# An attention and mixture-of-experts layer on one core: who rounds the posts' weights, the order of the last batch's units, and a written order for the end

## The chip, the cores and the metric

One Trainium2 chip, one of its cores. The metric is the device time of one execution in microseconds. PE is the tensor engine, DVE the vector engine, ACT the scalar engine, POOL (Pool) the GpSimd engine, SP the engine whose queue issues all the DMAs.

## The reference

Four sequences (batches) of 2048 tokens with 256 channels, in float32. Cut to what matters:

```
x = x + attention(layernorm(x))      # 16 heads of 16 channels; scale 1/16; + b_o + layernorm(x)
x = x + ffn(layernorm(x))
ffn(y): scores = softmax(y @ w_gate.T)               # 8 experts in 4 groups of 2
        two groups, then the two best experts inside them, by scores + expert_bias
        routed row r = token of expert index flat_idx[r], scaled by its weight
        h = silu(row @ w1[e]) * (row @ w3[e]); routed_out = h @ w2[e]
        shared = silu(y @ sw1.T) * (y @ sw3.T) @ sw2.T
        out = shared.at[flat_idx].add(routed_out)    # flat_idx are expert numbers, 0 to 7
```

As `flat_idx` holds expert numbers, the routed part reads rows 0 to 7 of the input and adds to rows 0 to 7 of the output alone. So it comes down to sums over all 16384 choices (two for each of 8192 tokens) of a sigmoid of a row's scaled product, weighted, for eight rows and eight experts.

## The kernel before, in words

The tokens are cut into chunks of 512, four to a batch, and the heads into four groups of four. A *unit* is one batch, one group and one chunk of queries against all 2048 keys of its batch; there are 64. A unit needs three streams on PE:

- the *maxima*: 64 products `mx` of 128 queries by 512 keys, each reduced by DVE to a row maximum `ms` (`mx_stream`, `finish_mx`). The negated maxima are transposed and sent by DMA into row 63 of the unit's query tile `qst`, where they act as an offset;
- the *scores*: 64 products `st` of 128 keys by 512 queries, each followed by ACT's exponential into `et` (`do_s`);
- the *values*: 16 steps of four products `av` (`do_a`), whose 17th row a head is the sum of the exponentials.

Maxima run about 1.4 units ahead of the scores; a unit's scores need all of its maxima. Queries and keys are split into a high and a low rounded part, so that a product in the fast format keeps its precision. Keys of one batch and group (2 MB) lie in one of two tiles `kst`, values in `vst`, queries in one of three `qst`; `load_unit` and `load_v` issue the loads. In the first three batches the units go group by group, so that one key load serves four units. In the last batch the first three chunks go group by group, and then the fourth chunk goes through all groups, with a third place for keys made of four other tiles (`spare_k`).

Beside the units runs other work: layer norms and projections of the next batch (`norm`, `qkv`: `pt_x`, `pp`, `pv`), and a *post* for each finished chunk (`post`: `post_first` divides by the sums, `post_a` makes the output product `po`, residual, second layer norm and its transpose `pt_x`; `route` makes gate products `lgT` and the ranking on DVE; `shared` makes `pa`, `pb`, `pd`). Each of these is a generator that yields what it needs. A planner orders PE, DVE, POOL and ACT while the program is built: it keeps an estimated clock for each engine (`plan.clock`), holds a window of the next steps, and improves their order by a seeded random search; `LATE` sets how much a late post costs in that search, for the last so many units of work. SP's queue is ordered by the framework.

`setup` loads the posts' four weights (`wt`, into two buffers) and splits them: ACT rounds the high part, POOL subtracts for the low part.

After the last unit, `last_heads` turns the last four heads, and `finish` alternates two generators, `front` (post_a of the last chunk, `route`, then the experts, `moe`) and `behind` (`post_b`, the shared part of the last chunk). Only their emission is alternated; the framework's scheduler orders the engines. `moe` counts choices (`m_cs`, `m_pc`, `m_tot`, `m_cum`), then goes through 16 groups of choices. For a group: `ob` and `ow` (the choice's one-hot rows, DVE and POOL), `mo` and `oT` (turned by PE, copied by DVE), `mu` (products with the tables), `mth` (their sigmoid: half by four ACT instructions, half by DVE and one ACT instruction), and `pg` (weighted sums in one bank). A step of the loop does ob, ow, mo and oT of group g, mu and mth of g-1, pg of g-2. Then `m_sg`, `m_ph`, `m_gb`, `m_pr`, `m_s`, `m_po`, and the last write.

Nearly every instruction is issued through one helper, line 56, so the profile's groups are told apart by tile names.

Of the kernel before, what the change touches and what calls it, by code (L numbers as in the profile page):

```python
# [33 lines left out]
LEAD = 6  # L34
HORIZON = 46
COMMIT = 10
LATE = 0.01, 0.1, 16
TURNS = 1600
WARM = 1.5
NET = 6  # L40
# [366 lines left out]
def body(tc, B, L, cols, x, wqkv, bqk, wst, bst, bv, wo, bo, wg, w1, w2, w3, sw1, sw2, sw3, ebias, cst, pad, out):  # L407
# [21 lines left out]
    def need(kind, ns=0, *tiles, more=0, act=940):  # L429


        return kind, ns, tiles, more, act

    def gate(open_):

        return "g", open_, (), 0, 0
# [123 lines left out]
    def to_channels(src, name, keep=None, fast=False, out=None):  # L560

        h, l = out or hl(f"t_{name}")
        if not fast:
            for c in range(2):
                f = keep[:, c, :] if keep is not None else sb.tile([P, QC], F32, tag="qkf", name=f"f_{name}{c}", bufs=2)
                pt = stile(f"pt_{name}{c}")
                for i in range(TQ):
                    T.transpose(pt[:, i * P:(i + 1) * P], src[:, i, c * P:(c + 1) * P], ident)
                S.copy(f, pt)
                G.tensor_copy(h[:, c, :], f)  # L570
                G.tensor_tensor(l[:, c, :], f, h[:, c, :].bitcast(F32), ALU.subtract)
                if c == 0:
                    yield need("s1", 436, act=470)
            return h, l
        for c in range(2):
            pt = mtile(f"pt_{name}{c}")
            for i in range(TQ):
                T.transpose(pt[:, i * P:(i + 1) * P], src[:, i, c * P:(c + 1) * P], ident)
            S.copy(keep[:, c, :], pt)
# [250 lines left out]
    def moe():  # L830
# [17 lines left out]
        pg = ps_av.tile([P, QC], F32, tag="av", name="pg")  # L848
        GR = 8
        NG = NR // GR  # L850
        ows, oTs, ths = {}, {}, {}

        def ranges(r0, r1):
            n = r1 - r0
            V.tensor_tensor(ge[:, r0:r1], K["rows"][:, r0:r1].unsqueeze(2).broadcast_to([P, n, E + 1]),
                            cum[:, 0:E + 1].unsqueeze(1).broadcast_to([P, n, E + 1]), ALU.is_ge)
            V.tensor_tensor(oe[:, r0:r1], ge[:, r0:r1, 0:E], ge[:, r0:r1, 1:E + 1], ALU.subtract)

        def pick(g):
            sl = slice(g * GR, (g + 1) * GR)  # L860
            ob = sb.tile([P, GR, E, 8], BF16, tag="x", name=f"ob_{g}", bufs=2)
# [5 lines left out]
            obf = ob.rearrange("p r e j -> p (r e j)")  # L867
            for q in range(GR // 2):
                T.matmul(pt[:, q * P:(q + 1) * P], obf[:, q * P:(q + 1) * P], identb, start=True, stop=True)
            oT = oTs[g] = sb.tile([P, GR // 2, P], F32R, tag="hi", name=f"oT_{g}", bufs=3)  # L870
            V.tensor_copy(r2(oT), pt)
# [56 lines left out]
    def post_first(b, c, nh=H):  # L928
# [63 lines left out]
    last = {}  # L992

    def post_last():

# [67 lines left out]
            V.tensor_tensor(xv, pd, xv, ALU.add)  # L1063
        write(ch, x1)

    def post_b(ch, n, x1, x2T, x2hl, rt, eng=G, hhl=None):

        hT = f4(f"hT_{n}")
        hhl = hhl or hl(f"hT_{n}")
        for m in range(2):  # L1070
            pa = mtile(f"pa_{n}_{m}")
            mm3(pa, W["s_1"], x2hl, slice(m * P, (m + 1) * P), slice(0, QC))
            th = sb.tile([P, QC], F32, tag="sth", name=f"th_{n}_{m}", bufs=2)
            S.activation(th, pa, AF.Tanh, scale=0.5)
            if eng is G:
                yield
            if eng is None:
                S.copy(hT[:, m, :], pa)
                G.tensor_tensor(th, th, K["ones"][:, 0:1].broadcast_to([P, QC]), ALU.add)
                G.tensor_tensor(th, th, hT[:, m, :], ALU.mult)  # L1080
            else:
                V.scalar_tensor_tensor(th, th, 1.0, pa, ALU.add, ALU.mult)
            yield
            next(rt, None)
# [3 lines left out]
            if eng is None:  # L1088
                S.mul(hT[:, m, :], pb, 0.5)
                G.tensor_tensor(hT[:, m, :], hT[:, m, :], th, ALU.mult)  # L1090
            else:
                V.scalar_tensor_tensor(hT[:, m, :], pb, 0.5, th, ALU.mult, ALU.mult)
            S.copy(hhl[0][:, m, :], hT[:, m, :])
            (eng or G).tensor_tensor(hhl[1][:, m, :], hT[:, m, :], hhl[0][:, m, :].bitcast(F32), ALU.subtract)
            yield
            next(rt, None)
# [12 lines left out]
    def spare(i):  # L1109

        t = kst[1 - kslot[kset[-1]]][:, i // 2, (i % 2) * 2 * QC:(i % 2 + 1) * 2 * QC]
        return t.rearrange("p (t n) -> p t n", t=2)

    def post(b, c):
# [9 lines left out]
    def finish():  # L1124
# [6 lines left out]
        def behind():  # L1131
            while "q" not in last:
                yield
            yield from post_b(*last["q"], iter(()), None)

        live = [front(), behind()]
        while live:
            for g in list(live):
                try:
                    next(g)  # L1140
                except StopIteration:
                    live.remove(g)


    queue, posts, side, norms, sums, firsts = (deque() for _ in range(6))
# [23 lines left out]
    def load_unit(u):  # L1169

        b, g, c = units[u]
        if fresh[u] and u != len(units) - 3:
            src = kd[b][4 * g:4 * g + 4].rearrange("(p h) r n -> (h r) p n", p=2)
            if kslot[kset[u]] == 2:
                spare_k.extend(hl("k_hq", "hq"))
                spare_k.extend(sb.tile([P, 2, QC], F32R, tag="x", name=f"k_x{i}", bufs=2) for i in range(2))
# [241 lines left out]
    def setup():  # L1418
# [359 lines left out]
```

## Time and profile before

| | |
|---|---|
| median of 3 runs | 3067.62 us (3067.2 to 3068.33) |
| profiled execution, its own time | 3064.53 us |
| its span, first to last instruction | 3062.7 us |
| mean granted PE clock | 0.986 |
| busy: PE, DVE, ACT, POOL | 2982.9, 2823.3, 2420.8, 649.9 us |
| last maximum reduced / last unit's exponentials begin | about 2931 / 2936.7 us |
| last value product ends / last group's pg ends | 2971.1 / 3056.6 us |

The busy times are unions of the instructions' spans on an engine; a matmul's end is modelled and matmuls overlap, so PE's share is not its share of peak. Stretches in the profile are cut in microseconds from the start of the span. The scores of unit 48 begin at 2251.9, of unit 52 at 2445.3, of unit 58 at 2685.9.

### The profile page before, as it was taken

The page shows a single profiled execution, that of the slowest core. Times are in us where ns is not written, and L with a number is a line of the kernel's source. Part 1 is how long each engine was busy: PE and PEld are TensorE (multiplying, and loading weights), DVE is VectorE, ACT ScalarE, POOL GpSimd, SP SyncE. Part 2 cuts the span into 40 slices and gives each one's busy share as a digit, 9 for nine tenths or more (in the row PEclk, how much of TensorE's full clock was granted, in tenths as well). Part 3 has the DMA queues.
Part 4 walks back from the last instruction along what each step waited for, and adds up shares of the span by engine and source line. Part 5 has one row for each costly group of instructions (what it writes and reads, how often), then busy time and mean ns, then how long its engine had stood idle before and what let it go on. Part 6 is the DMA issues. An engine that isn't in the chain of part 4 may idle for free.

```text
span 3062.7 us, 52745 instructions
## 1 busy us (share of the span) xinstructions
PE 2982.9 (97%) x19427; PEld 1359.8 (44%) x19427; DVE 2823.3 (92%) x5129; ACT 2420.8 (79%) x4745; POOL 649.9 (21%) x662
## 2 busy tenths in 40 slices
PE   7989999999999999999999999999999999999988
PEld 5434444444444444444444444444444444444436
DVE  7879999999999999999999999999999999999926
ACT  5578888888878878788888778888778788887774
POOL 5233223133213112110221220000222200023313
PEclk9899999999999999999999999999999999999998
DMA  5555645343121312221121200201121101011200
GB/s 157 184 156 151 167 114 162 94 140 112 51 94 40 115 32 88 64 79 69 44 86 39 72 25 20 90 22 69 45 75 49 69 25 58 31 54 40 77 26 15
DMA packets 144797, 237.32 MB, mean 77 GB/s; under 512 B 17115, under 2 KB 73563, under 8 KB 140379
## 3 DMA queue, kind: packets, MB, share of 16 engines
q1 hardware_dynamic: 144539, 233.96, 24.3%
q8 instruction: 153, 2.51, 0.3%
q14 instruction: 105, 0.86, 0.1%
HBM read 138.38 MB, written 111.80 MB: 82 GB/s over the span
## 4 chain that ended last, share of the span: by engine, by line
PE 80%; DVE 15%; DMA 1%; issue 1%; ACT 1%; POOL 1%; SPq 0%; POOLq 0%; ACTq 0%; DVEq 0%
PE av L56 29%; PE mx L56 20%; PE st L56 19%; DVE ms L56 11%; PE pp L56 3%; PE pd L56 2%; PE pv L56 1%; PE po L56 1%; PE pt_x L56 1%; PE pa L56 1%; PE pb L56 1%; PE mu L56 1%; ACT et L56 1%; PE pg L56 1%; DVE eq L56 1%
## 5 line engine op out<-in xcount | busy, mean ns | idle before, releaser
L56 DVE TENSOR_REDUCE ms<-mx 128x1 f32<-128x512 f32 x4096 | 2521.6, 682 | 135.0 <-PE mx L56 100.5
L56 ACT ACTIVATE et<-st 128x512 f32<-128x512 f32 x4096 | 2139.9, 611 | 440.4 <-PE st L56 288.2
L56 PE MATMUL mx<-kst,qst 63*128 63x512 f32 x3984 | 1222.7, 442 | 27.9 <-ACT et L56 10.6
L56 PE MATMUL st<-qst,kst 64*128 64x512 f32 x4032 | 1221.9, 440 | 7.3 <-DMA qst<-mt 3.4
L56 PE MATMUL av<-et,vst 128*32 128x512 f32 x8192 | 1098.4, 607 | 0.8 <-ACT ao L56 0.6
L56 PEld LDWEIGHTS mx<-kst,qst 63*128 63x128 f32 x3984 | 577.7, 186 | 605.8 <-DVE ms L56 289.8
L56 PEld LDWEIGHTS st<-qst,kst 64*128 64x128 f32 x4032 | 580.8, 186 | 556.1 <-DVE ms L56 278.9
L56 PEld LDWEIGHTS av<-et,vst 128*32 128x32 f32 x8192 | 164.0, 108 | 328.4 <-issue 307.7
L56 POOL TENSOR_TENSOR aT<-aT,rb 128x512 f32<-128x512 f32 (+1 forms) x32 | 40.9, 1285 | 571.3 <-DMA rb<-rd 570.9
L56 POOL CAST hi<-qkf 128x512 fp32r<-128x512 f32 x56 | 34.2, 610 | 328.3 <-ACT qkf L56 314.3
L56 POOL TENSOR_TENSOR lo<-qkf,hi 128x512 fp32r<-128x512 f32 x64 | 82.1, 1283 | 22.9 <-ACT hi L56 13.2
L56 ACT ACTIVATE qkf<-pp,b_qk 128x512 f32<-128x512 f32 x64 | 44.0, 687 | 53.8 <-PE pp L56 53.6
L56 POOL TENSOR_TENSOR th<-th,cs 128x512 f32<-128x512 f32 x32 | 33.5, 1046 | 222.8 <-ACT th L56 222.8
L56 POOL TENSOR_TENSOR rs_b<-rs_b,nhalf 128x4 f32<-128x4 f32 x16 | 16.3, 1017 | 279.7 <-DVE rs_b L56 279.7
L56 POOL TENSOR_TENSOR hT<-hT,th 128x512 f32<-128x512 f32 x32 | 41.0, 1281 | 123.7 <-ACT hT L56 47.4
L56 POOL TENSOR_TENSOR x<-x,xl 128x256 f32<-128x256 f32 x64 | 46.4, 755 | 16.8 <-ACT xl L56 16.8
L56 POOL TENSOR_TENSOR x<-x,b_o 128x256 f32<-128x256 f32 x64 | 45.5, 740 | 0.0
L56 ACT ACTIVATE xl<-x,rs_a 128x256 f32<-128x256 f32 x64 | 33.4, 594 | 11.1 <-DVE rs_a L56 11.0
L56 ACT COPY ao<-av 128x512 f32<-128x512 f32 x63 | 37.9, 601 | 3.0 <-PE av L56 2.0
L56 POOL TENSOR_TENSOR th<-th,sg 128x512 f32<-128x512 f32 x30 | 38.9, 1296 | 2.4
L56 ACT ACTIVATE th<-pa 128x512 f32<-128x512 f32 x32 | 19.2, 599 | 24.5 <-PE pa L56 24.2
L56 ACT ACTIVATE x<-x,rs_b 128x256 f32<-128x256 f32 x64 | 33.2, 597 | 6.6 <-DVE rs_b L56 6.6
(406 smaller groups left out, 2177.3 us busy)
## 6 DMA issues: line engine op xcount, KB each, us to landing
kst<-kd SPq DMA_DIRECT2D x16, 2048.0 KB
qst<-qd SPq DMA_DIRECT2D x63, 512.0 KB
qd<-hi SPq DMA_DIRECT2D x64, 256.0 KB
kd<-hi SPq DMA_DIRECT2D x64, 256.0 KB
ad<-ao SPq DMA_DIRECT2D x63, 256.0 KB
vst<-vd SPq DMA_DIRECT2D x19, 664.0 KB
vd<-vt SPq DMA_DIRECT2D x32, 332.0 KB
x<-x SPq DMA_DIRECT2D x16, 512.0 KB
```

What stands on the lines that cost most here:

```text
L56: r = f(*a, **k)
```

## The change

Five parts.

1. `split` with an engine given lets that engine (POOL) round the high part too. `setup`, and `post_first` ahead of its reciprocal, first pass a gate `later()`: nothing goes on until the planner's PE clock has moved by 12 us.
2. The last batch's units go chunk by chunk, four groups each. Every unit then needs other keys than the one ahead, and the places for keys go 0, 2, 1, 0, 2, 1 and so on. There are 16 key sets in the last batch.
3. `LATE` counts for the last 3 units of work, not 16.
4. `finish` runs in the written order on POOL, DVE, PE and ACT. `post_b` does its products and ACT's parts first; its ten POOL operations wait until the experts' loop has begun, and go one to a step. The transposes' low parts (`low`) come later, after the gate products. The copy of `m_cum` is taken out of its bank as `m_cm`.
5. The experts' loop has four stages: step g does pg of g-3, ob and ow of g, mu and mth of g-2, mo and oT of g-1. `ow` shares the six buffers of `et`.

```diff
-LATE = 0.01, 0.1, 16
+LATE = 0.01, 0.1, 3
...
+    def later(ns=12000):
+        t = plan.clock["PE"] + ns
+        return gate(lambda: plan.clock["PE"] > t)
...
     def split(name, tmp, out=None, eng=None):
-        S.copy(h, tmp)
+        (S.copy if eng is None else eng.tensor_copy)(h, tmp)
         (eng or V).tensor_tensor(l, tmp, h.bitcast(F32), ALU.subtract)
...
     def to_channels(src, name, keep=None, fast=False, out=None):      # its fast part
+        pts = []
         for c in range(2):
-            pt = mtile(f"pt_{name}{c}")
+            pts.append(mtile(f"pt_{name}{c}"))
...
-            S.copy(h[:, c, :], pt)
-            V.tensor_tensor(l[:, c, :], pt, h[:, c, :].bitcast(F32), ALU.subtract)
-            yield
+            S.copy(keep[:, c, :], pts[c])
+        for c in range(2):
+            S.copy(h[:, c, :], pts[c])
+        def low():
+            for c in range(2):
+                V.tensor_tensor(l[:, c, :], pts[c], h[:, c, :].bitcast(F32), ALU.subtract)
+        last["low"] = low
+        yield
...
+        cm = sb.tile([P, E + 1], F32, tag="m_cm", name="m_cm", bufs=1)
+        V.tensor_copy(cm, cum[:, 0:E + 1])
...
-            ow = ows[g] = sb.tile([P, GR, E, 8], F32, tag="lo", name=f"ow_{g}", bufs=3)
+            ow = ows[g] = sb.tile([P, GR, E, 8], F32, tag="et", name=f"ow_{g}", bufs=6)
...
+        def turn(g):                    # mo and oT, out of pick
...
-        for g in range(NG + 2):
+        for g in range(NG + 3):
+            last["at"] = g
             if g % STEP == 0 and g < NG:
                 ranges(g * GR, min(NR, (g + STEP) * GR))
+            if g >= 3:
+                gather(g - 3)
             if g < NG:
                 pick(g)
+            if 2 <= g < NG + 2:
+                hidden(g - 2)
             if 1 <= g <= NG:
-                hidden(g - 1)
-            if g >= 2:
-                gather(g - 2)
+                turn(g - 1)
...
+        yield later()                   # post_first
         yield need("d", 480, s1)
         V.reciprocal(s1, s1)
...
-    def post_b(ch, n, x1, x2T, x2hl, rt, eng=G, hhl=None):
+    def post_b(ch, n, x1, x2T, x2hl):
+        g2 = sb.tile([P, 2, QC], F32, tag="et", name=f"g2_{n}", bufs=6)
...
         for m in range(2):
...
+            S.activation(ths[m], pa, AF.Tanh, scale=0.5)
+            S.copy(hT[:, m, :], pa)
...
+            S.mul(g2[:, m, :], pb, 0.5)
             yield
+        while last["at"] < 0:
+            yield
+        for m in range(2):
+            G.tensor_tensor(ths[m], ths[m], K["ones"][:, 0:1].broadcast_to([P, QC]), ALU.add)
+            yield
+            G.tensor_tensor(ths[m], ths[m], hT[:, m, :], ALU.mult)
+            yield
+            G.tensor_tensor(g2[:, m, :], g2[:, m, :], ths[m], ALU.mult)
+            yield
+            G.tensor_copy(hhl[0][:, m, :], g2[:, m, :])
+            yield
+            G.tensor_tensor(hhl[1][:, m, :], g2[:, m, :], hhl[0][:, m, :].bitcast(F32), ALU.subtract)
+            yield
...
+        with tc.manual_schedule(engines={ENG.Pool, ENG.DVE, ENG.PE, ENG.Activation}):    # finish
+            while live:
...
-    units += [(B - 1, g, c) for g in (3, 2, 1, 0) for c in range(NPER - 1)] + [(B - 1, g, NPER - 1) for g in range(4)]
+    units += [(B - 1, g, c) for c in range(NPER) for g in range(4)]
...
-    kslot[-3:] = kslot[-5], 2, kslot[-4]
+    for k in range(4 * (B - 1), len(kslot)):
+        kslot[k] = (0, 2, 1)[(k - 4 * (B - 1)) % 3]
...
-        if fresh[u] and u != len(units) - 3:
+        if fresh[u]:
...
             t = load_w(src, "sth", 2)                                  # setup
-            yield need("a", 530, t)
+            yield later()
+            yield need("p", 2600, t)
             W[n] = split(n, t, eng=G)
```

More of the change, by code (lines that the diff above doesn't have):

```diff
@@ L574, in to_channels @@
             return h, l
+        pts = []
         for c in range(2):
-            pt = mtile(f"pt_{name}{c}")
+            pts.append(mtile(f"pt_{name}{c}"))
             for i in range(TQ):
-                T.transpose(pt[:, i * P:(i + 1) * P], src[:, i, c * P:(c + 1) * P], ident)
-            S.copy(keep[:, c, :], pt)
-            S.copy(h[:, c, :], pt)
-            V.tensor_tensor(l[:, c, :], pt, h[:, c, :].bitcast(F32), ALU.subtract)
-            yield
+                T.transpose(pts[c][:, i * P:(i + 1) * P], src[:, i, c * P:(c + 1) * P], ident)
+            S.copy(keep[:, c, :], pts[c])
[6 more added lines that the diff above has]
+        yield
         return h, l
@@ L850, in moe @@
         NG = NR // GR
-        ows, oTs, ths = {}, {}, {}
+        obs, ows, oTs, ths = {}, {}, {}, {}
         def ranges(r0, r1):
@@ L855, in ranges @@
             V.tensor_tensor(ge[:, r0:r1], K["rows"][:, r0:r1].unsqueeze(2).broadcast_to([P, n, E + 1]),
-                            cum[:, 0:E + 1].unsqueeze(1).broadcast_to([P, n, E + 1]), ALU.is_ge)
+                            cm.unsqueeze(1).broadcast_to([P, n, E + 1]), ALU.is_ge)
             V.tensor_tensor(oe[:, r0:r1], ge[:, r0:r1, 0:E], ge[:, r0:r1, 1:E + 1], ALU.subtract)
@@ L860, in pick @@
             sl = slice(g * GR, (g + 1) * GR)
-            ob = sb.tile([P, GR, E, 8], BF16, tag="x", name=f"ob_{g}", bufs=2)
-            ow = ows[g] = sb.tile([P, GR, E, 8], F32, tag="lo", name=f"ow_{g}", bufs=3)
+            ob = obs[g] = sb.tile([P, GR, E, 8], BF16, tag="x", name=f"ob_{g}", bufs=2)
+            ow = ows[g] = sb.tile([P, GR, E, 8], F32, tag="et", name=f"ow_{g}", bufs=6)
             ee = oe[:, sl, :].unsqueeze(3).broadcast_to([P, GR, E, 8])
@@ L865, in pick @@
             G.tensor_tensor(ow, ee, oj[:, sl, :].unsqueeze(2).broadcast_to([P, GR, E, 8]), ALU.mult)
+        def turn(g):
             pt = mtile(f"mo_{g}")
-            obf = ob.rearrange("p r e j -> p (r e j)")
+            obf = obs.pop(g).rearrange("p r e j -> p (r e j)")
             for q in range(GR // 2):
@@ L990, in post_a @@
         return ch, n, x1, x2T, x2hl
-    last = {}
+    last = {"at": -1}
     def post_last():
@@ L1064, in shared @@
         write(ch, x1)
-    def post_b(ch, n, x1, x2T, x2hl, rt, eng=G, hhl=None):
-        hT = f4(f"hT_{n}")
-        hhl = hhl or hl(f"hT_{n}")
+    def post_b(ch, n, x1, x2T, x2hl):
+        hT, hhl = f4(f"hT_{n}"), hl(f"hT_{n}")
+        g2 = sb.tile([P, 2, QC], F32, tag="et", name=f"g2_{n}", bufs=6)
+        ths = [sb.tile([P, QC], F32, tag="sth", name=f"th_{n}_{m}", bufs=2) for m in range(2)]
         for m in range(2):
@@ L1072, in post_b @@
             mm3(pa, W["s_1"], x2hl, slice(m * P, (m + 1) * P), slice(0, QC))
[L1073 to L1084, printed above, removed]
+            S.activation(ths[m], pa, AF.Tanh, scale=0.5)
+            S.copy(hT[:, m, :], pa)
             yield
@@ L1087, in post_b @@
             mm3(pb, W["s_3"], x2hl, slice(m * P, (m + 1) * P), slice(0, QC))
[L1088 to L1094, printed above, removed]
-            yield
-            next(rt, None)
+            S.mul(g2[:, m, :], pb, 0.5)
+            yield
+        while last["at"] < 0:
[10 more added lines that the diff above has]
+            G.tensor_tensor(hhl[1][:, m, :], g2[:, m, :], hhl[0][:, m, :].bitcast(F32), ALU.subtract)
             yield
@@ L1109, in spare @@
     def spare(i):
-        t = kst[1 - kslot[kset[-1]]][:, i // 2, (i % 2) * 2 * QC:(i % 2 + 1) * 2 * QC]
+        t = kst[0][:, i // 2, (i % 2) * 2 * QC:(i % 2 + 1) * 2 * QC]
         return t.rearrange("p (t n) -> p t n", t=2)
@@ L1133, in behind @@
                 yield
-            yield from post_b(*last["q"], iter(()), None)
-        live = [front(), behind()]
[L1137 to L1142, printed above, removed]
+            for _ in range(3):
+                yield
+            last["low"]()
+            yield
+            yield from post_b(*last["q"])
+        live = [front(), behind()]
+        with tc.manual_schedule(engines={ENG.Pool, ENG.DVE, ENG.PE, ENG.Activation}):
+            while live:
+                for g in list(live):
+                    try:
+                        next(g)
+                    except StopIteration:
+                        live.remove(g)
     queue, posts, side, norms, sums, firsts = (deque() for _ in range(6))
@@ L1171, in load_unit @@
         b, g, c = units[u]
-        if fresh[u] and u != len(units) - 3:
+        if fresh[u]:
             src = kd[b][4 * g:4 * g + 4].rearrange("(p h) r n -> (h r) p n", p=2)
             if kslot[kset[u]] == 2:
-                spare_k.extend(hl("k_hq", "hq"))
-                spare_k.extend(sb.tile([P, 2, QC], F32R, tag="x", name=f"k_x{i}", bufs=2) for i in range(2))
+                if not spare_k:
+                    spare_k.extend(hl("k_hq", "hq"))
+                    spare_k.extend(sb.tile([P, 2, QC], F32R, tag="x", name=f"k_x{i}", bufs=2) for i in range(2))
                 for i in range(4):
```

## The prediction

> **What bounds the kernel now.** I read the shares and slices of the page first, then its costliest groups, then the busy time in stretches cut at the score stream's units, then the waits of single engines and the chain at the end.
>
> ```profile
> PE 2982.9 (97%) x19427; PEld 1359.8 (44%) x19427; DVE 2823.3 (92%) x5129; ACT 2420.8 (79%) x4745; POOL 649.9 (21%) x662
> ...
> DVE  7879999999999999999999999999999999999926
> ...
> L56 DVE TENSOR_REDUCE ms<-mx 128x1 f32<-128x512 f32 x4096 | 2521.6, 682 | 135.0 <-PE mx L56 100.5
> ```
>
> PE shows 97%, but its matmuls overlap, so I weigh DVE: 64 units of 64 row maxima make its row of 2521.6 us. The stretches (us, PE, PEld, DVE, ACT, POOL busy, clock) say what a unit costs:
>
> ```profile
> 2606.90:2646.90 40.00, 39.93 (x258) 16.50 (x257) 39.45 (x67) 33.58 (x66) 0.00 (x0) 1.00 0.07 22
> 2727.30:2785.00 57.70, 54.16 (x338) 23.70 (x337) 53.28 (x100) 40.27 (x79) 21.67 (x19) 0.97 0.14 44
> 2785.00:2835.30 50.30, 49.91 (x323) 23.50 (x319) 48.91 (x98) 39.78 (x78) 16.12 (x15) 1.00 0.16 49
> 2835.30:2885.80 50.50, 48.48 (x329) 21.89 (x329) 48.52 (x90) 36.83 (x72) 10.43 (x10) 0.97 0.28 92
> 2885.80:2936.70 50.90, 46.03 (x298) 19.87 (x298) 37.81 (x72) 36.98 (x74) 12.84 (x10) 0.99 0.12 40
> 2936.70:2971.10 34.40, 34.40 (x196) 11.12 (x194) 0.55 (x1) 31.68 (x64) 6.18 (x6) 0.92 0.10 33
> 2971.10:3062.70 91.60, 69.39 (x573) 52.34 (x573) 57.98 (x107) 38.76 (x100) 29.06 (x27) 0.85 0.04 13
> ```
>
> A unit without posts takes 40.0 us with DVE idle 0.55. So the time is DVE's work, plus DVE's idle time up to its last maximum (2931), plus 40 us of exponentials that need that maximum, plus a tail of 91.6. The number of DVE instructions ahead of the last maximum is the same in both kernels. So I price only DVE's idle time and the tail.
>
> **Weights rounded by Pool.** Waits of ACT around the loading of the posts' weights, then those of DVE:
>
> ```profile
> ACT s_3h L56 <- DMA wt<-sw: 6.9, 1, 6.9
> ...
> ACT s_1h L56 <- DMA wt<-sw: 1.7, 1, 1.7
> ```
>
> ```profile
> DVE ms L56 <- PE mx L56: 13.6, 9, 8.2
> DVE ms L56 <- PE st L56: 1.9, 1, 1.9
> ```
>
> ACT stands 8.6 us in front of weights that have not landed; the exponentials are queued behind it, PE runs out of buffers, and DVE loses 15.5 us between 183 and 241. Ordinary idle time there is 2.0 in 23 us (stretch 232 to 255: DVE 20.97), so 5 of 58. The gain is 15.5 - 5 = 10.5; ACT's wait alone says 8.6, and the two weight loads on the critical chain 6.66 + 6.25 = 12.9. I take 11. In the built order the four casts (0.61 each) now stand on Pool, each behind a gate of 12 us of the planner's clock, which covers the longest wait seen. Queued behind them on Pool are the next chunk's rs_a and the hi/lo casts; Pool is 21% busy and those keys are a batch early, so 0 is lost; if the cover is gone, up to 6.9. SP's next weight load waits for Pool's split, and now stands behind the queries' writes. The same gate before the posts' reciprocal costs 0: DVE waited for that load once, 7.1 us, after its last maximum.
>
> **Last batch by chunks.** DVE's idle time in the four rows from 2727.3 is 4.4 + 1.4 + 2.0 + (13.1 - 5.7 after 2931) = 15.2; three posts crowd into units 58 to 62. With 0.5 for each of six more units, units 52 to 62 hold 18. In batch 2, units 45 to 51 (2116.9 to 2445.3, 328.4 us, DVE 319.4) idle 9.0 with four posts: 7 x 0.5 + 4 x 1.4. In the changed order the posts' matmuls stand in units 52-54, 56-58 and 60-61, none in 62: 11 x 0.5 + 3 x 1.4 = 9.7. Gain 8; bounds 0 (the idle time belongs to the stream's end, not to the crowd) and 13. The weight of lateness, now for three units, changes which order the search finds: I take 0, with 3.5 each way (some fifty units at 0.5 each, independent).
>
> Twelve more key loads of 2 MB are added. GB/s in 40 slices of 0.6 us, from the issue of one at 2076:
>
> ```profile
> GB/s 0 106 137 280 335 365 444 396 423 423 437 423 430 388 372 395 327 185 80 35 0 0 0 0 0 0 0 0 0 0 0 0 0 0 0 0 0 0 0 0
> ```
>
> It has landed, with the values behind it, after 12 us. In the changed order a load is freed by the previous unit's last score, when the maxima are 0.4 of a unit into the next; its first reader comes 0.6 of a unit, 23 us, later. Cover 11 us; cost 0. SP gets 35 more issues of about 0.4 us, beside everything.
>
> **The end, after the last value product (2971.1).** PE, DVE, ACT and POOL now keep the written order. (1) Both residual halves are added before the statistics: four pairs at 0.56 after 2978.4, so rs_b is 1.1 later. (2) lgT is no longer cut up by pa and pb: rs_b 2980.9, its Pool and DVE steps 1.3, four x to 2984.35, the second transposes and their copy to 2985.8, lgT's second half 0.65, lg, mx and sc 0.75, then DVE does the two low parts while ACT does the exponential: sm starts at 2988.6 instead of 2991.9. (3) From sm to wgt took 12.5; seven small DVE operations there lasted 0.66 to 1.42 beside Pool's work, 6.5 over their medians elsewhere. Pool now waits for wgt first, so 6.0: wgt at 2994.6. (4) m_pc stands behind 24 pa/pb matmuls: five or six left at 2988.05 plus 18, at 0.43 for about 5 us, then 0.235: 2995.8. m_cum starts at 2996.6 instead of 2996.6 + 10.4 = 3007.0. (5) The sixteen groups. The chain shows a group as it ran, and the last one with nothing to overlap:
>
> ```profile
> 3046.24 0.33 PE mo L56 x4
> 3046.57 1.00 PE mu L56 x8
> 3047.57 1.02 PE pg L56 x16
> ...
> 3053.29 1.16 PE mu L56 x8
> ...
> 3054.54 0.70 DVE mth L56
> ...
> 3055.27 0.64 ACT mth L56
> ...
> 3055.95 0.68 PE pg L56 x8
> ```
>
> Before, PE did the next group's mu while a group's sigmoid ran: 2.35 a group. In the changed order PE has mu, mo, then the same group's pg: only mo (0.33) lies in between, so the last row's serial path counts, 3053.29 to about 3056.47: 3.18. From m_cum: 5.2 to the first mu (before 5.6), 15 x 3.18 + 3.34 = 51.0, two groups at the low clock 1.4 (eight mu 0.213 apart, not 0.117), three ranges (0.75 each, two thirds in DVE's slack) 1.0, the two pd products that now stand in the loop 1.1 (twelve at 0.117, 0.8 of it in the wait for the sigmoid): 59.7, so 3056.3 against 3056.6. The tail gains 0.3. Bounds: -7 (2.75 a group, if the sigmoid ends with mo) and +16 (next paragraph).
>
> The clock: after 4.5 us without matmuls it was 0.50 from 2982 to 2990.2, and it came back 5.4 to 5.8 us after steady work began, but with gaps of 0.4 to 0.7 us it stayed:
>
> ```profile
> 3012.00:3017.30 5.30, 5.30 (x26) 4.19 (x26) 4.02 (x7) 2.00 (x6) 0.80 (x1) 0.50 0.00 0
> 3017.30:3026.00 8.70, 7.06 (x51) 5.13 (x50) 5.91 (x12) 2.38 (x9) 1.05 (x1) 0.99 0.01 2
> ```
>
> The new loop's gap is 0.6, so I take full clock. At half clock mu costs 0.7 and mo and pg 0.3 more: 16 x 1.0 = 16. The Trainium skill (TensorE: Matmul & The Clock Gate, "A second HAM failure mode: psum-queue depth-cycling") says the opposite of this row, that frequent short idles between matmul groups make the gate swing; by it the sum would be the half-clock one, 3064.
>
> Ten Pool operations now run beside DVE's ob. At 3028.72 Pool's ow took 1.05 and ob, 1.39, ended 0.55 after it. From oT's slot (2.5 into a group) ob may last 2.0 before the next mth; 1.3 + 0.55 fits, cost 0. The Trainium skill (SBUF — State Buffer, "SBUF: two separate sides") calls the port an exclusive lock held for the whole operation; by it ob takes its full 0.68 after Pool's 1.3, 2.0, and the slack is just used up.
>
> **Sum.** -11 - 8 - 0.3 = -19.3 on the profiled execution's 3064.5: 3045.2. The median of the runs lies 3.1 above that execution, so 3048.
>
> **Rivals.** (a) Spreading saves nothing, since DVE's work is the same; only ACT's wait goes: 3056. For: plain units idle 0.5, there is little to fill; against: 13.1 idle in one row. (b) Pool inherits the wait with the casts behind it, and the projections are late: 3059. For: Pool's order; against: the 12 us gate. (c) The experts' loop runs at half clock or otherwise 1 us longer a group: 3064, no change. (d) Slower: keys land late. Every unit of the last batch now waits for its own keys, 15 loads; a landing over 23 us stalls PE, DVE behind it. It eats the whole gain at 1.3 us late and shows as slower at 1.7; at 3 it is 3048 + 45 = 3093. Against: 12 us seen, and 4.7 MB after 2248.8 done in some 19.
>
> **How the numbers follow.** Forecast 0.55, (a) 0.18, (b) 0.10, (c) 0.10, (d) 0.07. A measurement tells about 0.2%, 6 us. The forecast, (a) and (b) are faster: 0.83; (c) is the same: 0.10; (d) is slower: 0.07. The forecast's own bounds, start 8.6 to 12.9, batch 0 to 13, tail -7 to some of +16, order 3.5, taken together, give 3038 to 3057; with (a) and (b) up to 3060.
>
> **What would show it.** Right: no wait of ACT on wt; DVE idle near 5 between 183 and 241 of before; the last value product ends near 2952; m_cum 10 us earlier after it; 3.2 a group at clock 1.00. Wrong: Pool waits on wt with DVE waits behind; maxima waiting on DMA after 2250; clock 0.50 beyond 3010; a tail over 95.

## The result, and the profile after

The changed kernel takes 3073.65 us (median of 18 runs, 3070.32 to 3081.38), the kernel before 3067.03 (18 runs): ratio 1.0023, interval 1.0016 to 1.0030. It is slower by 6.6 us where 19 us less were predicted (3048, at most 3060). The profiled execution took 3075.23 (span 3073.1), 1.6 above its median; that of before lies 2.5 below its own. So the two traces differ by 10.4 where the medians differ by 6.6, and stages are compared with several profiles of one order at hand.

The page of the changed kernel, the rows shown of before:

```profile
PE 2993.7 (97%) x19427; PEld 1361.4 (44%) x19427; DVE 2819.1 (92%) x5130; ACT 2418.0 (79%) x4739; POOL 657.1 (21%) x668
...
DVE  7799999898999999999999999999999999999925
...
L56 DVE TENSOR_REDUCE ms<-mx 128x1 f32<-128x512 f32 x4096 | 2519.4, 680 | 137.2 <-PE mx L56 98.8
```

DVE's work is the same; its idle time ahead of maxima is 137.2 instead of 135.0, though the prediction took 19 us out of DVE's idle time. Where it sits is read from stretches cut at the maxima: units 0 to 3, units 4 to 47, units 48 to 63, then to the last value product, then the tail (columns: stretch, length, busy PE, PEld, DVE, ACT, POOL, clock, DMA). Length less DVE busy is DVE's idle time. Before:

```profile
0.00:238.35 238.35, 204.14 (x1082) 110.33 (x1083) 187.91 (x343) 152.30 (x289) 92.07 (x110) 0.92 0.53 167
238.35:2186.36 1948.01, 1938.19 (x12778) 861.87 (x12777) 1858.93 (x3352) 1606.08 (x3146) 381.96 (x398) 1.00 0.26 81
2186.36:2931.98 745.62, 735.46 (x4801) 323.39 (x4799) 717.50 (x1326) 591.39 (x1147) 140.62 (x122) 1.00 0.16 51
2931.98:2971.09 39.11, 35.70 (x203) 11.90 (x198) 0.98 (x3) 32.26 (x65) 6.18 (x6) 0.91 0.11 36
2971.09:3062.67 91.58, 69.40 (x573) 52.35 (x573) 57.98 (x107) 38.76 (x100) 29.06 (x27) 0.85 0.04 13
```

The changed kernel:

```profile
0.00:230.51 230.51, 202.91 (x1093) 112.25 (x1094) 189.07 (x343) 151.25 (x288) 92.27 (x112) 0.93 0.53 168
230.51:2193.26 1962.75, 1945.36 (x12766) 856.84 (x12762) 1864.25 (x3348) 1604.15 (x3141) 382.17 (x397) 1.00 0.26 80
2193.26:2938.90 745.64, 736.16 (x4804) 325.01 (x4803) 712.32 (x1330) 592.11 (x1150) 143.24 (x124) 1.00 0.27 88
2938.90:2978.47 39.57, 35.32 (x195) 11.54 (x195) 0.98 (x3) 32.09 (x65) 6.24 (x6) 0.91 0.11 35
2978.47:3073.07 94.60, 73.90 (x575) 55.72 (x575) 52.52 (x108) 38.41 (x98) 33.14 (x30) 0.87 0.04 12
```

The first four units gain 7.8. Units 4 to 47, in which the change moves almost no work, lose 14.7: that is the surprise. The last batch is level (DVE idles 5 more and is busy 5 less). The tail loses 3.0. The rest is 0.5.

Waits of ACT in the changed kernel, from 150 to 300 us (engine, what waited, for what: us, times, longest). The weights are gone from them, as predicted:

```profile
ACT et L56 <- PE st L56: 7.2, 17, 0.9
ACT qkf L56 <- PE pp L56: 7.0, 8, 1.3
ACT et L56 <- PE mx L56: 4.7, 9, 1.1
ACT vt L56 <- PE pv L56: 1.6, 3, 0.9
```

Two groups of the experts' loop in the changed kernel's chain (start, us, what): nothing of PE lies between mu and pg but mo, and a group takes 3.31 us (3022.29 to 3025.60):

```profile
3022.29 1.16 PE mu L56 x8
...
3023.54 0.70 DVE mth L56
...
3024.26 0.64 ACT mth L56
...
3024.95 0.66 PE pg L56 x8
3025.60 1.16 PE mu L56 x8
```

### The profile page after: what moved, and what is told of

It reads as the page before. It is cut to its first block, busy times and chain, and to the rows that moved or that the text cites. A ratio compares the mean times of both kernels' runs of the same rounds, so it can differ in the third digit from the quotient of the medians.

```text
span 3073.1 us, 52849 instructions
## 1 busy us (share of the span) xinstructions
PE 2993.7 (97%) x19427; PEld 1361.4 (44%) x19427; DVE 2819.1 (92%) x5130; ACT 2418.0 (79%) x4739; POOL 657.1 (21%) x668
## 4 chain that ended last, share of the span: by engine, by line
PE 77%; DVE 17%; issue 2%; DMA 1%; ACT 1%; POOL 1%; SPq 0%; POOLq 0%; DVEq 0%; ACTq 0%
PE av L56 27%; PE st L56 19%; PE mx L56 18%; DVE ms L56 12%; PE pp L56 3%; PE pd L56 2%; PE pv L56 1%; PE po L56 1%; PE pt_x L56 1%; PE pa L56 1%; PE pb L56 1%; DMA qd<-hi 1%; DVE gt L56 1%; ACT et L56 1%; DVE eq L56 1%
## 5 line engine op out<-in xcount | busy, mean ns | idle before, releaser
L56 DVE TENSOR_REDUCE ms<-mx 128x1 f32<-128x512 f32 x4096 | 2519.4, 680 | 137.2 <-PE mx L56 98.8
L56 PE MATMUL st<-qst,kst 64*128 64x512 f32 x3776 | 1141.2, 441 | 14.0 <-DMA qst<-mt 6.7
L56 PE MATMUL mx<-kst,qst 63*128 63x512 f32 x3728 | 1133.0, 441 | 19.5 <-DVE ms L56 11.3
L56 PEld LDWEIGHTS st<-qst,kst 64*128 64x128 f32 x3776 | 538.6, 185 | 562.6 <-DVE ms L56 281.8
L56 PEld LDWEIGHTS mx<-kst,qst 63*128 63x128 f32 x3728 | 535.1, 186 | 526.9 <-DVE ms L56 266.4
L56 PE MATMUL st<-qst,k_x 64*128 64x512 f32 x160 | 53.9, 454 | 0.6 <-DVE ms L56 0.3
L56 PE MATMUL mx<-k_x,qst 63*128 63x512 f32 x160 | 49.9, 439 | 0.5 <-DVE ms L56 0.3
```

What stands on the lines that cost most here:

```text
L56: r = f(*a, **k)
```

## Experiments: one part at a time

First three of the parts, each alone on the kernel before; then two more edits of the end. The gate in `post_first` was not run alone.

**Setup alone** (e1_setup): `split` lets Pool round, and `setup` has its two gates; `post_first` has none.

> Only the posts' weights rounded by Pool behind the 12 us gate (no gate in post_first, all else as before). Theory A (every part acts where its edit stands, as the two traces read): no wait of ACT on wt; DVE's idle time in the first four units of maxima 49.6 us before, 40.5 in the changed kernel, so about 9 less, and units 12 to 26 stay near the 32 us of before: about 3058, -9. The prediction's term: -11, 3056. Theory B (the order search starts from another state and finds another order for every later unit; the 12 us that the changed kernel lost in units 12 to 26 are the luck of that draw, not an edit): the first four units gain 9 all the same, but units 12 to 26 may hold anything from 28 to 45, so the time lies anywhere from 3054 to 3071.

3073.02 us, ratio 1.0015 (1.0006 to 1.0024): slower. Yet DVE's idle time in units 0 to 3 is 39.5, 11 below before's 50.4 (stretches cut as above; the expectations count it some 0.8 lower). Units 4 to 47 took 1958.9 instead of 1948.0, units 48 to 63 749.9 instead of 745.6. The gain is there, and more is lost later, where nothing was edited. The changed kernel has the same idle times within 0.2 from unit 3 to unit 14 (6.3 and 6.2 in unit 12, 3.3 in before): most of the loss in the middle came with the setup.

In unit 15 the two part: 8.7 us of idle time in the changed kernel, 2.8 here. Up to there DVE does the same instructions in the same order; what follows is the first post, which only the changed kernel holds back with a gate. The reciprocal of the sums `s` is written out and comes back as `rb`, by which Pool multiplies `aT`; from that `po` is made. The load of `s` was issued at 705.96 us in the changed kernel and at 703.31 here. First rows of the changed kernel, with DVE's wait for `po`, then of this run:

```profile
733.52 0.54 DVE L56 RECIPROCAL s<-s 128x64 f32<-128x64 f32 x1
748.12 1.29 POOL L56 TENSOR_TENSOR aT<-aT,rb 128x512 f32<-128x512 f32 x1 [9.73 <-DMA rb<-rd]
...
DVE x L56 <- PE po L56: 3.6, 1, 3.6
```

```profile
720.32 0.54 DVE L56 RECIPROCAL s<-s 128x64 f32<-128x64 f32 x1
...
732.72 2.53 POOL L56 TENSOR_TENSOR aT<-aT,rb 128x512 f32<-128x512 f32 x2
```

With the gate the reciprocal comes 27.6 us after the issue of its load and not 17.0; Pool then waits 9.7 us for `rb`, and DVE 3.6 us for `po`, with the maxima behind that wait in its queue. In this run DVE's longest wait for `po` between 690 and 2210 us is 0.2.

**Order of units alone** (e2_order): `units`, `kslot` and `load_unit`, nothing else.

> Only the last batch's units chunk by chunk with three places for keys; the order of PE is that of before up to about unit 46. The prediction's term: DVE's idle time in units 52 to 62 falls, -8, about 3059. Theory A (spreading the posts saves nothing and costs: a unit with a post idles 2.4 us wherever it stands, and the end of the stream starves all the same): DVE's idle time in units 52 to 62 rises from 13.2 to about 17 and unit 63 stays at 9.5 to 10.4: +5, about 3072. Late keys: waits of PE or DVE on loads of keys behind 2250, 3 us for each of 15 loads, 3110.

3075.95 us, ratio 1.0025 (1.0015 to 1.0034). DVE's idle time in units 48 to 63 is 40.1 instead of 28.1; 4.4 of it are two reciprocals of posts that waited for their load, which the gate in `post_first` was there for. No maxima waited for keys. The predicted saving is not seen.

**The written end alone** (e4_tail): the hunks of `to_channels`, `moe`, `post_b` and `finish`; the stream is before's.

> Only the written order of the end, with post_b's Pool steps inside the experts' loop and the four stages; the stream before the last value product is instruction for instruction that of before. The prediction's term: -0.3. Theory A: the tail is 94.6 us as in the changed kernel instead of 91.6, since a group takes 3.31 and not 2.35, and the early m_cum (10 us) is all spent by that: +3, about 3070. Theory C (the tail was slow in the changed kernel only because the stream before left the clock or a queue in another state): 91 to 92, no change.

3071.09 us, ratio 1.0008 (0.9999 to 1.0017), tail 94.43 against 91.58: the time is not told from before's, the tail is theory A's. Its profile repeats before's order up to the last value product, and so shows how far one order repeats: DVE's idle time by unit agrees within 0.3 us in 58 of the 64 units; units 0 to 3 gave 49.3 to 53.8 in nine profiles of that order.

**Another order of the loop** (e6_loop), on top of that:

```
-            if g >= 3:
-                gather(g - 3)
             if g < NG:
                 pick(g)
-            if 2 <= g < NG + 2: hidden(g - 2)
             if 1 <= g <= NG:
                 turn(g - 1)
+            if 2 <= g < NG + 2: hidden(g - 2)
+            if g >= 3:
+                gather(g - 3)
```

> As the run with the written end alone, but a step of the experts' loop does ow and ob of g, mo and oT of g-1, mu and mth of g-2, and only then pg of g-3, so that PE has the weighted sums of an older group and the next turn to do while a sigmoid runs. Theory A (the loop's order is what spends the gain): a group comes down from 3.31 to about 2.4, the tail from 94.6 to about 80, the whole to about 3056, -11. Rival D (Pool's work for the shared part holds DVE and the loop is bound by them): a group stays above 2.9, the tail at 88 or more, 3064 or more.

3060.19 us, ratio 0.9973 (0.9963 to 0.9983), tail 83.86, 4 us more than the 80 of theory A. The chain of this run; a group is 2.35 us again (3038.31 to 3040.66), for PE has pg of an older group to do while a sigmoid runs:

```profile
3037.30 1.00 PE mu L56 x8
3038.31 1.02 PE pg L56 x16
3039.33 0.33 PE mo L56 x4
3039.66 0.99 PE mu L56 x8
3040.66 1.02 PE pg L56 x16
```

**Buffers of their own for g2** (e18_loop_lo), on top of that. In the changed kernel the sigmoids of one group waited for Pool's last step on `g2`, 2.3 us: g2 has one (not two, as my expectation puts it) of the six buffers that ow and mth go round in.

```
-        g2 = sb.tile([P, 2, QC], F32, tag="et", ..., bufs=6)
+        g2 = [sb.tile([P, QC], F32, tag="lo", ..., bufs=3) for m in range(2)]
```

> As the run with the loop's order changed (pg last), and the half-scaled second gate products g2 in two buffers of their own instead of two of the six that the loop's ow and mth go round in. Theory (in that run and in the changed kernel the sigmoids once stood behind Pool's last step on g2, 3.6 us from 3023 to 3027, because their buffer was g2's): the wait of mth on hT_3l is gone and the tail falls from 83.9 to about 81. Rival (Pool itself is late with ow there, whichever buffer): the tail stays at 83 to 84.

3059.26 us, ratio 0.9970 (0.9960 to 0.9979); the wait is gone from the list and the tail is 81.98, 1.9 less in the profiles. Medians of e6_loop and this run cannot tell 1.9.

## Experiments: the order that the search draws

**Other seeds of the search** (e9_seed2, e12_seed3): `Random(1)` becomes `Random(2)` or `Random(3)` in the kernel before.

> The kernel before with one number changed: the order search starts its random draws from seed 2 instead of 1. No work, wait or place is changed. Theory B (the search's draw decides several us anywhere in the stream): the first four units keep 48 to 52 us of DVE's idle time, since there the edit-free cause stays, but units 4 to 62 (107 us of idle before) come out anywhere from 100 to 120 and the time from 3060 to 3080. Theory A (the draw is worth 1 or 2 us, the edits are what counts): 105 to 109 there, 3066 to 3069.

> As the run with seed 2, with seed 3. Theory B: another draw from the same spread, units 4 to 62 between 100 and 120 us of DVE's idle time. Theory A: 105 to 109, the time within 2 us of before.

3094.94 us (1.0095, 1.0082 to 1.0109) and 3083.15 us (1.0057, 1.0045 to 1.0070). The same work with another draw is 29 and 17 us slower than the kernel before beside them (3065.83). Theory B holds, and more strongly than it was put. The stretches of units 4 to 47 and 48 to 63, of seed 2 and then of seed 3:

```profile
238.27:2206.05 1967.78, 1950.36 (x12789) 860.02 (x12788) 1863.25 (x3353) 1605.81 (x3145) 380.65 (x397) 0.99 0.25 80
2206.05:2958.49 752.44, 739.71 (x4803) 325.46 (x4801) 717.53 (x1326) 590.87 (x1150) 143.32 (x124) 1.00 0.15 51
```

```profile
236.02:2186.21 1950.19, 1939.58 (x12787) 855.70 (x12783) 1857.51 (x3351) 1607.53 (x3146) 378.93 (x393) 1.00 0.25 80
2186.21:2941.95 755.74, 740.94 (x4801) 328.19 (x4797) 718.93 (x1328) 590.59 (x1150) 141.55 (x123) 0.99 0.15 50
```

Against 1948.0 and 745.6 both stretches are longer in both, though units 4 to 47 of seed 3 by 2.2 us alone, 0.3 beyond what before's own order has shown (1946.3 to 1949.9 in eight profiles). Seed 1 is a good draw for the kernel before; any edit that shifts the planner's clocks draws again.

**Setup alone and the whole change, with seed 2** (e10_setup_seed2, e19_after_seed2).

> Weights rounded by Pool in setup, alone, with seed 2. Theory B: the first four units idle about 39 us as in the run with seed 1 (49.6 before), and units 4 to 62 take another value than its 118: with a typical draw the time is 3055 to 3062, better than before, the setup's gain of 11 showing in full. Theory A, changed after that run (the earlier start itself makes the later units worse, whatever the draw): units 12 to 26 stay near 39 and not 32, and the time stays above 3068.

> The changed kernel with the order search's seed 2 instead of 1. Theory B (seed 1 is a good draw for the kernel before and an ordinary one for the changed kernel): the changed kernel moves little, DVE's idle time in units 4 to 63 stays in the band of the other new draws, 128 to 138 (131 with seed 1), so 3070 to 3080; against the kernel before with the same seed (3095) it is then some 20 us faster, near what was predicted. Rival (the changed kernel is slower by its edits): it is as far above before's seed 2 as it is above its seed 1, 3100.

3077.89 us and 3083.67 us. At seed 2 the setup edit is 17 us better than before (3094.94), the whole change 11 us better; the second is less than the 20 that I expected, and 3083.67 lies above my band, with units 4 to 63 idle 134.9. The first fits neither theory whole: the time is above 3068, where theory A put it, but units 12 to 26 fell back to 32.3, as theory B says, and the time was lost in units 48 to 63, which took 763.7. In units 4 to 47 the setup edit is 10.9 us longer than before at seed 1 (1958.9 against 1948.0) and 11.5 shorter at seed 2 (1956.3 against 1967.8): the sign goes with the draw and not with the edit. The gate in `post_first` does not change sign: the changed kernel is longer there than the setup alone by 3.9 at seed 1 and by 6.2 at seed 2 (1962.5 against 1956.3). So the spread between draws, 2 to 20 us in units 4 to 47, is larger than any part of the change.

**The weight of lateness** (e8_after16): the changed kernel with `LATE = 0.01, 0.1, 16`.

> The changed kernel with the weight of lateness again on the last 16 units of work instead of 3. Up to about unit 46 it is the changed kernel's order. Theory: chunk by chunk and a weight on 16 units do not go together, since each post is pressed into one unit: DVE's idle time in units 52 to 62 is 20 or more (17.3 in the changed kernel, 23.6 in the run with the order alone, of which 4.4 were reciprocals waiting for their load, which the gate removes): about 3076. Rival (the weight does nothing measurable): 17 to 18, 3073.

3074.09 us, units 48 to 63 745.7 against 745.6: my theory fell, the rival held. The weight does nothing that can be seen here.

**The setup with the order held** (e15_same_draw). The planner books the old cost and Pool gets the instruction, so the search draws the same: the sequences of PE and DVE are before's.

```
-        S.copy(h, tmp)
+        if eng is None:
+            S.copy(h, tmp)
+        else:
+            plan.book_act("copy", h, [tmp], {})
+            nc.gpsimd.tensor_copy(h, tmp)
```

> The kernel before with the four casts of the posts' weights on Pool, but the planner still books them on ACT and there is no gate: the order of PE, DVE and ACT is that of before, instruction for instruction, less the four casts. Theory B (the edit is worth 11 us; what the run with the setup alone lost again was the order drawn anew): DVE's idle time in the first four units falls from 48 to 52 to about 38, the later units stay at 116 to 119, and the time falls by 10 to 11: 3055 to 3057. Rival (b) of the prediction, which this order invites since no gate holds Pool back: Pool waits 7 to 9 us on wt and the casts and subtractions behind it come late; then the first four units stay above 44 and the time above 3061.

3066.98 us, ratio 0.9994 (0.9986 to 1.0003): nothing. Waits of Pool, then of DVE, in this run from 150 to 260 us:

```profile
...
POOL s_3h L487 <- DMA wt<-sw: 5.0, 1, 5.0
POOL s_1h L487 <- DMA wt<-sw: 4.9, 1, 4.9
POOL w_oh L487 <- DMA wt<-wo: 3.0, 1, 3.0
...
DVE rs_a L56 <- POOL rs_a L56: 8.2, 1, 8.2
```

This is the prediction's rival (b): without a gate Pool stands in front of the loads, the next chunk's rs_a is queued behind it, DVE waits 8.2 us for that, and the maxima are queued behind DVE's wait. So the move to Pool alone is worth nothing here; it takes the gate, or loads that come earlier.

**The loads first, order held** (e20_loads_first): as the run before, and nobody has to wait.

```
+        two = [sb.tile([P, 2, 2, D], F32, tag="x1", ..., bufs=2) for i in range(2)]   # unused until the first post
+        wts = [two[i // 2][:, i % 2] for i in range(4)]
+        for t, (n, src) in zip(wts, ws):
+            nc.sync.dma_start(t, src)
         for ...:
-            t = load_w(src, "sth", 2)
+            plan.book_sp("dma_start", t, [src], {})
             yield need("a", 530, t)
```

> The kernel before with the four loads of the posts' weights issued one after the other at the start of setup, into two tiles that lie unused until the first post, and their casts on Pool, booked by the planner as before: the order of PE and DVE is that of before, instruction for instruction, and nobody waits for wt. Theory B: DVE's idle time in the first four units falls from 48 to 53 (four profiles of that order) to 38 to 40, the later units stay at 115 to 119, the time falls by about 10: 3057. Rival (something else then holds units 2 and 3, as Pool did in the run without a gate): 45 or more in the first four units, 3063 or more.

3056.96 us, ratio 0.9961 (0.9948 to 0.9973): 12.0 less. Its stretches of units 0 to 3, 4 to 47 and 48 to 63: the first lost 11.3 of its length, the second is before's, and the third, whose order is before's too, is 3.3 longer:

```profile
0.00:227.09 227.09, 199.70 (x1082) 108.76 (x1083) 188.14 (x344) 150.11 (x285) 94.52 (x114) 0.95 0.53 169
227.09:2175.23 1948.14, 1938.28 (x12778) 861.85 (x12777) 1858.18 (x3352) 1605.86 (x3146) 381.92 (x398) 1.00 0.26 81
2175.23:2924.16 748.93, 737.44 (x4801) 324.20 (x4799) 717.41 (x1326) 591.37 (x1147) 140.47 (x122) 0.99 0.15 51
```

With the order held, taking the wait for the weights away is worth what the prediction said.

**The last 16 units drawn again** (e22_group_re2, e23_group_re3 with the old order of units, e25_chunk_re2, e26_chunk_re3 chunk by chunk, without the gate): one line more in `present`, everything up to unit 46 as before.

```
+        if made > NS - 16 * NK and "re" not in last:
+            last["re"] = True
+            search.random = Random(2).random          # or 3
```

> The kernel before, whose search takes new random draws (seed 2) from unit 48 on. The order up to unit 46 is that of before. Theory B (the order of before is a lucky draw at the end too): DVE's idle time in units 48 to 63, 28 us in before, comes out at 32 to 38; the time is 4 to 10 above before. Theory A: 27 to 30.

> The last batch chunk by chunk (no gate, as in the run with the order alone), with new draws (seed 2) from unit 48 on. If the order of units costs nothing by itself: as the same draws with the old order of units, plus at most 4.4 of reciprocals waiting for their load: 32 to 42 us of DVE's idle time in units 48 to 63 (40 in the run with the order alone). If it costs by itself: above 42 again and again. If it saves the predicted 8: 24 to 30.

> As the run with the old order of units and new draws from unit 48 on, with seed 3. Theory (the order of before is a lucky draw there; an ordinary one takes some 755 us for units 48 to 63, busy and idle together, by the five redrawn runs so far, 750 to 764): 750 to 760, the time 4 to 12 above before. Rival (the first redraw was the exception): 745 to 748.

> As the run chunk by chunk with new draws from unit 48 on, with seed 3. Theory (by itself the order of units saves about 7, most of it in DVE's busy time, 710 to 716 us in units 48 to 63 against 716 to 726, because its ranking operations run beside less of Pool's work): 744 to 752 busy and idle together, 4 to 8 less than the pair's other run. Rival (no difference of its own): 750 to 760, equal to the pair's other run within 3.

They took 3077.80, 3069.03, 3073.52 and 3074.53 us (1.0035, 1.0001, 1.0015 and 1.0019 of before). Length of units 48 to 63, and DVE busy in it, for all the draws there are:

| units 48 to 63, us | old order of units | chunk by chunk |
|---|---|---|
| seed 1, as in before / in e2_order | 745.6, 717.5 | 751.9, 711.9 |
| redrawn from unit 48, seed 2 | 752.2, 721.7 | 745.1, 710.2 |
| redrawn from unit 48, seed 3 | 751.5, 716.1 | 749.5, 715.5 |
| redrawn from the start | 752.4, 755.7, 749.9, 763.7 | 745.6 (changed kernel), 745.7, 751.3 |

The mean of the six redrawn on the left is 754.3, of the six on the right, which are all new draws, 748.2. So in these profiles chunk by chunk seems worth some 6 us against an ordinary draw of the old order; but the pairs say -7.1 and -2.1, one draw moves a stretch by up to 14, before's one order took 745.0 to 748.9 in eight profiles, and before's own draw is as good as the best on the right. The medians of the whole runs say -8.8 and +1.0 for the two pairs, and e2_order is 8.4 slower than before. So neither the gain nor its size is settled, and what differs is partly DVE's busy time, not only its idle time. e22 came out better in idle time than I expected (30.5) and worse in busy time; the 34.9 of e25 lie where its expectation put an order of units that costs nothing by itself.

**What the runs point to** (e17_both, then e21_all): the held order and the written end with pg last and g2's own buffers; in e17_both with the casts as in e15_same_draw, in e21_all with the loads first. Neither has the chunk by chunk order or a gate.

> The order of before kept for the stream (casts of the posts' weights on Pool, booked as before), and the written end with pg last and g2 in buffers of its own; no chunk by chunk order, no gates. Theory: the two gains add: 11 from the first four units, 8 to 11 from the tail: about 3047. If the setup's gain is lost again as in the run with the setup alone, 3057.

> As the run with the loads issued first, and the written end with pg last and g2 in buffers of its own. Theory: 10 from the first four units and 10 from the tail (82 instead of 91.6): about 3047. Rival as for that run: 3054.

3055.19 us (0.9962, 0.9949 to 0.9976): the tail is 81.80, and units 0 to 3 idle 49.6 (50.4 in before), so the gain is the tail's, as e15_same_draw would have told. And 3041.62 us, ratio 0.9913 (0.9900 to 0.9927), 27 us below before and 32 below the changed kernel. The two gains add: units 0 to 3 are 9.9 shorter than before's, the tail 8.0. The 27 are more than the 20 that the traces show, whose profiled execution is the slowest of the four (3045.27).

## Why the prediction was wrong

Between the two traces the sum missed by 29.7 us: 14.7 in units 4 to 47, which it put at 0, 8.0 in the last batch, 3.3 in the tail, 3.2 in the first four units, 0.5 elsewhere.

The step that failed first is a half sentence: that the change "changes which order the search finds: I take 0, with 3.5 each way". I worked out 3.5 as if fifty units drew anew around the old mean. But before's order is not an ordinary draw: of six draws anew in units 4 to 47 (setup alone with two seeds, before with two, the changed kernel with two) all six were longer than 1948.0, by 2.2 to 19.8, 11.7 on average, while eight profiles of the old order lie between 1946.3 and 1949.9. Of the changed kernel's 14.7, 10.9 came with the setup alone, and this part is the draw: at seed 2 the same edit made the stretch shorter, and with the order held it is before's (1949.9 in e15_same_draw, 1948.1 in e20_loads_first).

The other 3.9 came with a second term that I put at nothing: "The same gate before the posts' reciprocal costs 0". I had asked only whether the reciprocal waits for its load, not who waits for the reciprocal. At the first post the gate made DVE wait 3.6 us for `po` (4.5 in e8_after16, whose order is the same there), and unit 15 idles 5.9 more than in e1_setup. At seed 2 no wait of DVE for `po` in units 14 to 47 is over 0.5. How much of the 3.9, and of the 6.2 at seed 2, is the gate and how much the order that it draws anew, no run separates.

- **Weights rounded by Pool, -11:** right in its mechanism. 12.0 less by time in e20_loads_first, and 8 to 11 of idle time in units 0 to 3 wherever the gate stood. The price "if the cover is gone, up to 6.9" was too low: without cover the whole gain goes (e15_same_draw).
- **Last batch, -8:** as a difference to before it was 0.0 in the traces (745.64 against 745.62). Rival (a), that spreading saves nothing, describes it: a unit with a post idles about 2.4 and not my 1.4, and the stream's end starves as much (10.4 in unit 63 against 9.5). I had also read the rows from 2727.3 as crowded posts: by the maxima, units 52 to 62 of before idle 13.5 and not the 18 of the sum, and the 9.5 of unit 63, which no run made smaller, were in my 15.2. Against an ordinary draw the order may be worth something; that is not settled.
- **Keys:** right. No unit waited for them; rival (d) did not occur.
- **The end, -0.3:** it lost 3.0. After the last value product rs_b came at 9.96 (predicted 9.8), m_cum at 26.5 (25.5), the first mu at 30.85 (30.7). The loop from there took 57.65 and not 54.5. Its first two groups took 9.66 (7.76 predicted), with a table load of ACT, 1.28, on the chain ahead of the first sigmoid (in before it ran at 3001.29, 12.5 ahead of it). The other fourteen took 48.0 (46.8): a group was 3.31, not 3.18, as the path from mu to the end of pg has 0.13 more of handing over than I counted, and one (3035.47 to 3039.41) was 3.94 for g2's buffer; the ranges cost nothing.
- **The clock:** right for the loop. It came back later than in before: 0.50 until about 3018.4, 9.1 us after the first mu (5.4 to 5.8 in before), as the mean of 0.91 from 3017 to 3025 shows. Then, with a gap in every group, it stayed full, here from 3050 to 3066 in the changed kernel:

```profile
3050.00:3066.00 16.00, 14.85 (x138) 11.38 (x132) 7.80 (x13) 8.63 (x25) 2.11 (x2) 1.00 0.10 34
```

The Trainium skill (TensorE: Matmul & The Clock Gate, "A second HAM failure mode: psum-queue depth-cycling") would have had the clock swing under such gaps; this row does not show it, and rival (c) did not occur. The page speaks of a swing between half and full clock, so my 3064, half clock throughout, was the most that could follow from it.

- **ob beside Pool:** right. The changed kernel's order of instructions by time, a product of Pool and ob:

```profile
3027.86 1.27 POOL L56 TENSOR_TENSOR g<-g,th 128x512 f32<-128x512 f32 x1
3028.06 1.62 DVE L56 TENSOR_TENSOR ob<-m_oe,oh 128x512 bf16<-128x512 bf16 x1
```

ob starts 0.2 after Pool and ends 0.55 after Pool's end, and mth, the next on DVE, still had 0.49 to wait for mu. The Trainium skill (SBUF — State Buffer, "SBUF: two separate sides") calls the port a lock for the whole operation; by it ob would have ended 0.69 after Pool, the length of the ob at 3032.21 that began ahead of Pool's ow (which then took 1.47, not 1.05). So the rows agree but for 0.14.

With seed 2 on both sides the change gives -11.3, its parts being about -8.5 (units 0 to 3), -5 (units 4 to 47, the draw), -1 (48 to 63) and +3.6 (the tail) in the traces. So the sum was nearer to this pair of draws than to the pair that there was. But before's draw at seed 2 is the longest of all in units 4 to 47. Over all the seeds run, before took 3067, 3095 and 3083 us and the changed kernel 3074 and 3084: whether the change gains against an ordinary draw is not settled.

## What to carry to other kernels

Where an order comes from a seeded search, an edit is two edits: its own and a new draw. Price the first with the order held (book the old cost, change the instruction), and the second with a few seeds of the unchanged kernel, before adding either to a sum; a kernel whose seed was good loses that luck with any edit that draws anew. An engine freed of a wait has only handed it on if the load is as late as before: issue the load earlier, or see what is queued behind the new waiter. A gate that spares one engine a wait makes everything behind the gated step later: follow that step to its last reader. In a loop of stages, put work of another group on the engine between a product and the consumer of its sigmoid; adding a stage without that makes the path serial.

## What the runs showed of the hardware

One order repeats closely from run to run: DVE's idle time in units 4 to 47 was 88.4 to 91.5 us in eight profiles. The small ranking operations of DVE, 177 to 180 of them in units 48 to 63 without two of over 2 us, lasted 0.25 us on average while Pool was idle and 0.56 while it was busy (130 and 47 of them in before; 0.24 and 0.65, 152 and 28 of them, in the changed kernel): together 58.8 and 53.7 us, which is the 5 us of DVE's busy time in which the last batch differs.
